# Attention probabilities moved in 32-partition blocks: the order of the block transfers and the length of their pieces

## The chip, the cores and the metric

The kernel runs on one core of a Trainium2 chip. Five engines work beside each other there: TensorE (PE) for matrix products, VectorE (DVE), ScalarE (ACT), GpSimd (POOL) for elementwise work, and SyncE (SP), which in this kernel only issues transfers. The transfers themselves (DMAs) are carried out by 16 DMA engines that all queues share. The metric is the device time of one launch in microseconds; a kernel's time is the median of several runs.

## What is computed

A transformer layer on 8 sequences of 512 tokens with 256 features, all in float32: the normed input goes both through attention with 16 heads of 64 and through a mixture of 16 experts, and both results are added to the input.

```python
xn = _layernorm(x)
# attention, per head
q, k = rope(q), rope(k)
kb = -p * log1p(a * abs(pos_k - pos_q))
attn = softmax(q @ k.T / 8 + kb)
out = (attn @ v) heads joined @ out_w.T
# experts: each token goes to its best one, at most 256 tokens each
h = relu(dispatched @ w1[e]); expert_out = h @ w2[e]
x + attention + gate * expert_out[token]
```

## The kernel before

The attention runs in 32 steps, `s`. A step is a group of four heads (`g = s // 8`) on one sequence (`b = s % 8`), and it falls into two pairs of heads. Each pair is worked in four units of 128 queries (`qc`), two units to a loop body; the body's number is `d`, so a pair takes two bodies. The order of all instructions is written out by hand in the loop over `d` from line 850 on; nothing is reordered afterwards. Each engine, and SyncE's queue of transfers, executes its instructions strictly in that order.

For one pair the data goes this way. `score` (line 610) multiplies queries and keys on PE, adds the distance bias on DVE (line 631) and exponentiates on ACT (line 635). The result stays in a tile `z` with queries on the partitions. The product with the values needs keys on the partitions, so the probabilities must be transposed. `turn` (line 640) does that within blocks of 32 by 32, on DVE. What is left is to move whole blocks between groups of 32 partitions, and this is done by transfers in `move` (line 646): 16 of them for a pair, one for each pair of a source group `qi` and a destination group `g`, from `z` to a tile `pt`. All 16 are issued on SyncE. After the first four a small transfer stores the softmax's reciprocal sums to DRAM (`rd`), and after all 16 two more load them back, broadcast (`rb`). Two pairs later `attend` (line 708) multiplies `pt` with the values, and `attended` (line 720) scales by `rb`. The very last pair is transposed on PE instead (`turn_last`, line 673), so there are 63 moves with 1008 block transfers in all.

Before the change a `z` tile holds, within a partition, first the head of the pair `j`, then the key group `g`, then the key block `c`, then the query unit `qc`, then 32 numbers. A block transfer therefore finds, in each of its 32 source partitions, two pieces of 512 numbers (2048 bytes), one for each head. `pt` is laid out the same way.

SyncE's queue carries more than the blocks. In each step it also loads the partial output (`y`, line 736) and stores it (`yd` or `out`, line 742), loads the normed input two steps ahead (`xnT`, line 235), and during the experts' stage loads their weights (`w`, lines 471 and 480) and stores their results (`eo`, line 538). At the end of a step's second body `load_normed` is called just before `move`. The other queue of transfers, GpSimd's, carries gathers and the first loads and stores.

The buffers: three `z` tiles, two `pt` tiles, two `xnT` tiles, two `y` tiles. A move can be issued when the last `turn` of its pair is done and the `pt` tile of two pairs before has been read by `attend`.

The stages in time: up to about 160 us start-up and norming, to 360 us attention alone with the routing of tokens, to about 1050 us attention with the experts' products in between, then attention with the gathering of the experts' results.

Of the kernel before, what the change touches and what calls it, by code (L numbers as in the profile page):

```python
# [9 lines left out]
F32 = mybir.dt.float32  # L10
# [3 lines left out]
ALU = mybir.AluOpType  # L14
# [3 lines left out]
B, S, DM, H, D = 8, 512, 256, 16, 64  # L18
E, F = 16, 1024
P = 128  # L20
NTOK = B * S
NT = NTOK // P
TB = S // P
# [3 lines left out]
GC = HG * D  # L27
XB = 2
KBW = 2 * S - P
ROT = [(i + 16) % 32 for i in range(32)]  # L30


@with_exitstack
def attention_and_experts(
# [13 lines left out]
    nc = tc.nc  # L48
# [11 lines left out]
    zpool = ctx.enter_context(tc.tile_pool(name="zpool", bufs=3))  # L60
    ptpool = ctx.enter_context(tc.tile_pool(name="ptpool", bufs=2))
# [62 lines left out]

    dist = const.tile([P, TB, KBW // P, 32], F32, name="dist")

    def bias_tables(g, pair, stage):

        for j in range(2):
            h = g * HG + 2 * pair + j  # L130
            if stage == 0:
                kb[h] = kbpool.tile([P, TB, KBW // P, 32], F32, tag="kb", name=f"kb_{h}")
                nc.scalar.activation(
# [16 lines left out]
    for i in range(2):  # L150
# [11 lines left out]
    nc.gpsimd.iota(  # L162
        dist, pattern=[[32, TB], [P, KBW // P], [1, 32]], base=-(S - P),
        channel_multiplier=-1, allow_small_or_imprecise_dtypes=True,
# [399 lines left out]
    def project_qk(s, pair, part, turn_too=True):  # L564
# [8 lines left out]
        sh = rope.tile([P, S], F32, tag="sh", name=f"sh_{s}_{pair}_{part}", bufs=3)  # L573
        nc.vector.stream_shuffle(sh, ps, ROT)  # L574
        t = qkpool.tile([P, S], F32, tag=f"qk{part}{pair}", name=f"t_{s}_{pair}_{part}")
# [34 lines left out]
    def score(s, pair, qc):  # L610

        g = s // B
        q, k = qk[s, pair, 0], qk[s, pair, 1]
        if qc == 0:
            zts[s, pair] = zpool.tile([P, 2, TB, TB, TB, 32], F32, tag="z", name=f"z_{s}_{pair}")
            sums[s, pair] = small.tile([P, 2, TB], F32, tag="sums", name=f"sums_{s}_{pair}")
        sc = [ps_sc.tile([P, S], F32, tag="sc", name=f"sc_{s}_{pair}_{qc}_{j}") for j in range(2)]
        for j in range(2):
            r = slice(j * D, (j + 1) * D)
            nc.tensor.matmul(  # L620
                sc[j].rearrange("p (g c k) -> p g c k", g=TB, k=32),
                q[r, qc * P : (qc + 1) * P],
                k[r, :].rearrange("p (c g k) -> p g c k", g=TB, k=32),
                start=True, stop=True,
            )
        st = small.tile([P, 2], F32, tag="st", name=f"st_{s}_{pair}_{qc}")
        for j in range(2):
            z = zts[s, pair][:, j, :, :, qc, :]
            bias = kb[g * HG + 2 * pair + j][:, :, TB - 1 - qc : 2 * TB - 1 - qc, :]

            nc.vector.tensor_tensor_reduce(  # L631
                z, sc[j].rearrange("p (g c k) -> p g c k", g=TB, k=32), bias, -0.125, 3.0e38,
                ALU.add, ALU.min, st[:, j : j + 1],
            )
            nc.scalar.activation(  # L635
                z, z, AF.Exp, bias=st[:, j : j + 1], scale=-1.0,
                accum_out=sums[s, pair][:, j, qc : qc + 1],
            )

    def turn(s, pair, qc):  # L640

        for j in range(2):
            z = zts[s, pair][:, j, :, :, qc, :]
            nc.vector.transpose(z, z)  # L644

    def move(s, pair):


        z = zts.pop((s, pair))
        inv = inverse[(2 * s + pair) % 2]  # L650
        nc.vector.reciprocal(inv[:, : 2 * TB], sums.pop((s, pair)).rearrange("p j c -> p (j c)"))
        turned = small.tile([P, 32], F32, tag="turned", name=f"turned_{s}_{pair}", bufs=2)
        nc.vector.transpose(turned, inv)
        pt = ptpool.tile([P, 2, TB, TB, P], F32, tag="pt", name=f"pt_{s}_{pair}")
        rd = rdram.tile([TB, 32, 32], F32, tag="rd", name=f"rd_{s}_{pair}")
        for qi in range(TB):
            for g in range(TB):
                nc.sync.dma_start(  # L658
                    pt[g * 32 : (g + 1) * 32, :, qi].rearrange("p j c q -> p j (c q)"),
                    z[qi * 32 : (qi + 1) * 32, :, g].rearrange("p j c q k -> p j (c q k)"),  # L660
                )
            if qi == 0:
                nc.sync.dma_start(rd.rearrange("a c q -> (a c) q"), turned)
        rb = rope.tile([P, TB, P], F32, tag="rb", name=f"rb_{s}_{pair}")
        for j in range(2):
            nc.sync.dma_start(
                rb[j * D : (j + 1) * D],
                rd[:, j * TB : (j + 1) * TB, :].rearrange("a c q -> a (c q)").partition_broadcast(D),
            )
        pts[s, pair] = pt  # L670
        norms[s, pair] = rb

    def turn_last(s, pair, qc):

        if qc == 0:
            pts[s, pair] = zpool.tile([P, 2, TB, S], F32, tag="z", name=f"pt_{s}_{pair}")
        rs = small.tile([P, 2], F32, tag="rs", name=f"rs_{s}_{pair}_{qc}")
        nc.vector.reciprocal(rs, sums[s, pair][:, :, qc])
        for j in range(2):
            zn = rope.tile([P, S], F32, tag="sh", name=f"zn_{s}_{pair}_{qc}_{j}", bufs=3)  # L680
            nc.vector.tensor_scalar(
                zn.rearrange("p (c g k) -> p g c k", g=TB, k=32),
                zts[s, pair][:, j, :, :, qc, :], rs[:, j : j + 1], None, ALU.mult,
            )
            ps = ps_mm.tile([P, TB, P], F32, tag="mm", name=f"zt_{s}_{pair}_{qc}_{j}")
            for kc in range(TB):
                nc.tensor.transpose(ps[:, kc, :], zn[:, kc * P : (kc + 1) * P], ident)
            nc.scalar.copy(pts[s, pair][:, j, :, qc * P : (qc + 1) * P], ps)
# [19 lines left out]
    def attend(s, pair):  # L708
        avs[s, pair] = av = ps_av.tile([P, S], F32, tag="av", name=f"av_{s}_{pair}")
        for kc in range(TB):  # L710
            for j in range(2):
                c0 = pair * P + j * D
                nc.tensor.matmul(  # L713
                    av[j * D : (j + 1) * D, :].rearrange("p (a q) -> p a q", q=P),
                    vals[s][:, kc, c0 : c0 + D], pts[s, pair][:, j, :, kc, :],
                    start=(kc == 0), stop=(kc == TB - 1),
                )
        del pts[s, pair]
# [113 lines left out]
    turn_by(nc.vector, k0[2], k0[0], k0[1], slice(0, S))  # L832
    keep_warm(14)
    score(*units[0])
    score(*units[1])
    turn_by(nc.gpsimd, q0[2], q0[2], q0[1], slice(2 * P, S))
    bias_tables(0, 1, 1)
# [12 lines left out]
    for d in range(duos):  # L850
        s, dd = divmod(d, TB)
        g, b = divmod(s, B)
        pair, half = divmod(dd, 2)
# [5 lines left out]
        if d + 1 < duos:  # L859
            score(*units[2 * d + 2])  # L860
            score(*units[2 * d + 3])
        was = divmod((d - 5) // 2, 2) if half and d >= 5 else None
        if was:
            attend(*was)
# [16 lines left out]
        if d == duos - 1:  # L881
            attended(*was)
            project_out(s - 1, 0)
            project_out(s - 1, 1)
            store_y(s - 1, True)
        (turn_last if final else turn)(*units[2 * d])
        if was and d < duos - 1:
            attended(*was)
# [6 lines left out]
        if dd in (0, 1):  # L895
            project_v(s, dd)
        (turn_last if final else turn)(*units[2 * d + 1])
        if dd == 1 and 4 <= s + 2 < steps:
            load_normed(s + 2)
        if half and not final:  # L900
            move(s, pair)
# [44 lines left out]
        for bb in range(2):  # L946
            k = d - late - 6 * bb - 4
# [8 lines left out]
        for bb in (B - 2, B - 1):  # L956
            k = d - duos + 6 - (bb - B + 2)
# [14 lines left out]
        if b == 0 and g > 0 and dd == 0:  # L972
            bias_tables(g, 1, 1)
    attend(s, 0)
    attended(s, 0)
    for i2 in range(2):
# [56 lines left out]
```

## Time and profile before

| | us |
|---|---|
| median of 3 runs | 1273.08 |
| lowest and highest | 1268.95, 1273.43 |
| the profiled execution, its own time | 1280.13 |
| its span in the profile | 1278.4 |

The page of the profile gives the span in 40 slices; each digit is a share in tenths, 9 for 90% or more:

```profile
PE   8799999999999999999999999999999999999867
DVE  7998897999866556566556566655665568878762
PEclk9899998999999999999999999999999999999989
DMA  4589998888788898878786887877768768999985
```

It gives the transfers of each queue (packets, megabytes, and their time as a share of that of 16 engines), and the chain of work that ended last, by engine:

```profile
q1 hardware_dynamic: 177104, 240.98, 73.6%
q0 software_dynamic: 6368, 20.99, 6.0%
...
PE 71%; DMA 13%; DVE 6%; SPq 5%; ACT 3%; issue 1%; POOL 1%; ACTq 0%; DVEq 0%
```

Queue q1 is SyncE's, q0 GpSimd's. "SPq" is time of SyncE's own instructions, which only issue. The rows of issues read: what is moved, by which queue, how often, KB each, and the median time from issue to landing:

```profile
pt<-z SPq DMA_DIRECT2D x1008, 128.0 KB, 3.2
w<-in_w SPq DMA_DIRECT2D x64, 512.0 KB, 7.4
rb<-rd SPq DMA_DIRECT2D x126, 128.0 KB, 4.1
xnT<-xnd SPq DMA_DIRECT2D x28, 512.0 KB, 5.9
yd<-y SPq DMA_DIRECT2D x26, 512.0 KB, 5.2
y<-yd SPq DMA_DIRECT2D x24, 512.0 KB, 6.8
```

The block transfers are 1008 of about 1400 issues and half of all bytes that the queue moves (1008 x 128 KB of 241 MB).

### The profile page before, as it was taken

How to read it: one execution, taken by the hardware profiler on the slowest of the kernel's cores; microseconds unless marked ns; L12 is line 12 of the kernel's file. 1: busy time of each engine (PE TensorE's matmuls, PEld its weight loads, DVE VectorE, ACT ScalarE, POOL GpSimd, SP SyncE). 2: the span in 40 equal slices, each digit the busy share in tenths (PEclk: the TensorE clock that was granted, in tenths of full speed). 3: DMA queues.
4: the chain of work that ended last, by engine and by line, in shares of the span. 5: the costliest groups of instructions: out<-in, count | busy, mean ns of one | idle time of the engine just before them, and what ended most of it. 6: DMA issues, size and time to landing. Idle time of an engine off the chain costs nothing.

```text
span 1278.4 us, 17383 instructions
## 1 busy us (share of the span) xinstructions
PE 1219.7 (95%) x5070; PEld 670.1 (52%) x5070; DVE 893.5 (70%) x2265; ACT 611.7 (48%) x1425; POOL 617.4 (48%) x614
## 2 busy tenths in 40 slices
PE   8799999999999999999999999999999999999867
PEld 5344444444455565655556565555656554444434
DVE  7998897999866556566556566655665568878762
ACT  6566653466443343445533444443446435555551
POOL 5766654455543343334433344433435334686840
PEclk9899998999999999999999999999999999999989
DMA  4589998888788898878786887877768768999985
GB/s 133 144 209 245 263 229 211 199 199 207 198 221 211 235 238 234 210 198 212 205 217 166 240 203 213 222 209 193 188 195 214 198 156 200 209 227 228 214 229 143
DMA packets 184670, 264.15 MB, mean 207 GB/s; under 512 B 32176, under 2 KB 96448, under 8 KB 184576
## 3 DMA queue, kind: packets, MB, share of 16 engines
q1 hardware_dynamic: 177104, 240.98, 73.6%
q0 software_dynamic: 6368, 20.99, 6.0%
q10 hardware_dynamic: 1104, 1.07, 0.2%
q8 instruction: 41, 0.67, 0.2%
q14 instruction: 53, 0.43, 0.1%
HBM read 99.39 MB, written 31.44 MB: 102 GB/s over the span
## 4 chain that ended last, share of the span: by engine, by line
PE 71%; DMA 13%; DVE 6%; SPq 5%; ACT 3%; issue 1%; POOL 1%; ACTq 0%; DVEq 0%
PE sc L620 13%; PE qk L570 13%; PE av L713 12%; PE po L752 8%; PE v L597 8%; PE ph L515 8%; PE po L530 7%; DMA xnT<-xnd 5%; SPq L658 4%; DMA pt<-z 4%; DMA w<-in_w 3%; DVE z L631 2%; DVE z L644 1%; ACT z L635 1%; ACT xn L245 1%
## 5 line engine op out<-in xcount | busy, mean ns | idle before, releaser
L583 POOL TENSOR_TENSOR t<-t,cos_t 128x512 f32<-128x512 f32 (+1 forms) x126 | 161.3, 1280 | 556.0 <-ACT t L579 555.8
L635 ACT ACTIVATE z<-z,st 128x512 f32<-128x512 f32 x512 | 363.3, 711 | 44.8 <-DVE st L631 36.4
L631 DVE CUSTOM_DVE_ANT_1 z<-sc,kb 128x512 f32<-128x512 f32 x512 | 322.6, 686 | 35.3 <-PE sc L620 26.5
L644 DVE STREAM_TRANSPOSE z<-z 128x512 f32<-128x512 f32 x504 | 319.8, 682 | 0.0
L570 PE MATMUL qk<-xnT,wq 128*128 128x512 f32 x512 | 247.8, 607 | 12.6 <-DMA xnT<-xnd 8.1
L620 PE MATMUL sc<-t,t 64*128 64x512 f32 x1024 | 255.3, 617 | 0.7 <-DVE t L585 0.7
L713 PE MATMUL av<-pt,v 128*64 128x512 f32 x1008 | 235.5, 610 | 9.1 <-DMA pt<-z 8.3
L579 ACT COPY t<-qk 128x512 f32<-128x512 f32 x125 | 73.2, 585 | 341.8 <-DVE sh L574 341.8
L574 DVE LOAD_MASK_SELECT sh<-qk x128 | 1.8, 14 | 241.4 <-PE qk L570 239.4
L620 PEld LDWEIGHTS sc<-t,t 64*128 64x128 f32 x1024 | 88.5, 186 | 155.0 <-issue 127.7
L585 POOL TENSOR_TENSOR t<-t,sh 128x512 f32<-128x512 f32 (+1 forms) x126 | 160.5, 1274 | 9.9
L584 POOL TENSOR_TENSOR sh<-sh,sin_t 128x512 f32<-128x512 f32 (+1 forms) x126 | 161.0, 1278 | 0.0
L713 PEld LDWEIGHTS av<-pt,v 128*64 128x64 f32 x1008 | 69.2, 139 | 167.0 <-issue 136.6
L570 PEld LDWEIGHTS qk<-xnT,wq 128*128 128x128 f32 x512 | 94.4, 192 | 101.5 <-issue 69.0
L752 PE MATMUL po<-wo,o 128*128 128x256 f32 x512 | 124.3, 386 | 0.2 <-DVE o L723 0.2
L597 PE MATMUL v<-wq,xnT 128*128 128x256 f32 x512 | 124.1, 385 | 0.0
L530 PE MATMUL po<-w,hT 128*128 128x256 f32 x512 | 120.5, 383 | 3.5 <-DMA w<-in_w 2.5
L515 PE MATMUL ph<-xdT,w 128*128 128x256 f32 x512 | 118.8, 382 | 2.2 <-ACT eot L536 1.4
L752 PEld LDWEIGHTS po<-wo,o 128*128 128x128 f32 x512 | 94.5, 190 | 36.4 <-issue 11.1
L597 PEld LDWEIGHTS v<-wq,xnT 128*128 128x128 f32 x512 | 94.7, 190 | 35.8 <-DVE z L644 14.6
L515 PEld LDWEIGHTS ph<-xdT,w 128*128 128x128 f32 x512 | 95.6, 190 | 27.7 <-ACT z L635 4.9
L530 PEld LDWEIGHTS po<-w,hT 128*128 128x128 f32 x512 | 95.0, 190 | 28.7 <-issue 9.4
(147 smaller groups left out, 828.3 us busy)
## 6 DMA issues: line engine op xcount, KB each, us to landing
pt<-z SPq DMA_DIRECT2D x1008, 128.0 KB, 3.2
w<-in_w SPq DMA_DIRECT2D x64, 512.0 KB, 7.4
rb<-rd SPq DMA_DIRECT2D x126, 128.0 KB, 4.1
xnT<-xnd SPq DMA_DIRECT2D x28, 512.0 KB, 5.9
yd<-y SPq DMA_DIRECT2D x26, 512.0 KB, 5.2
y<-yd SPq DMA_DIRECT2D x24, 512.0 KB, 6.8
xrd<-xn POOLq DMA_DIRECT2D x8, 512.0 KB, 6.8
xnd<-xnT POOLq DMA_DIRECT2D x8, 512.0 KB, 7.8
```

The lines of the kernel that those rows point to most:

```text
L515: nc.tensor.matmul(ph[:, i, :], held["w1", e, fc // 4][:, mc, (fc % 4) * P : (fc % 4 + 1) * P], xdT[:, mc, :], start=(mc == 0), stop=(mc = ...
L530: nc.tensor.matmul(po[:, c, :], hT[:, fc, c * P : (c + 1) * P], held["w2", e, fc // 4][:, fc % 4, :], start=(fc == 0), stop=(fc == F // P ...
L570: nc.tensor.matmul(ps, wq[:, mc, c0 : c0 + P], xnTs[s][:, mc, :], start=(mc == 0), stop=(mc == 1),)
L583: eng.tensor_tensor(t[:, c], ps[:, c], cos_t[:, c], ALU.mult)
L584: eng.tensor_tensor(sh[:, c], sh[:, c], sin_t[:, c], ALU.mult)
L597: nc.tensor.matmul(ps[:, i, :], xnTs[s][:, mc, c0 : c0 + P], wq[:, mc, 2 * GC :], start=(mc == 0), stop=(mc == 1),)
L620: nc.tensor.matmul(sc[j].rearrange("p (g c k) -> p g c k", g=TB, k=32), q[r, qc * P : (qc + 1) * P], k[r, :].rearrange("p (c g k) -> p g c ...
L631: nc.vector.tensor_tensor_reduce(z, sc[j].rearrange("p (g c k) -> p g c k", g=TB, k=32), bias, -0.125, 3.0e38, ALU.add, ALU.min, st[:, j : ...
L635: nc.scalar.activation(z, z, AF.Exp, bias=st[:, j : j + 1], scale=-1.0, accum_out=sums[s, pair][:, j, qc : qc + 1],)
L644: nc.vector.transpose(z, z)
L713: nc.tensor.matmul(av[j * D : (j + 1) * D, :].rearrange("p (a q) -> p a q", q=P), vals[s][:, kc, c0 : c0 + D], pts[s, pair][:, j, :, kc, : ...
L752: nc.tensor.matmul(ps[:, i, :], oTs[pair][:, c0 : c0 + P], wot[:, pair, :], start=(pair == 0), stop=(pair == 1),)
```

## The change

The two layouts get the head `j` further inside, so that a block is one piece of 1024 numbers (4096 bytes) in each partition, in the source and in the destination. The 16 blocks are issued in a new order. Before, `qi` ran outside and `g` inside: eight transfers from the lower half of the partitions, then eight from the upper. Now a list names them by turns: (0,0), (2,2), (0,1), (2,3), (0,2), (2,0), (0,3), (2,1), and the same with 1 and 3 as sources. Every transfer reads from the other half than the one before it, and writes to the other half. The store of `rd` still follows the fourth block. All that reads or writes `z` and `pt` is indexed to suit; no operation is added or removed.

```diff
+BLOCKS = [
+    b for q in range(2) for g in range(4) for b in ((q, g), (q + 2, (g + 2) % 4))
+]
...
-            zts[s, pair] = zpool.tile([P, 2, TB, TB, TB, 32], F32, tag="z", name=f"z_{s}_{pair}")
+            zts[s, pair] = zpool.tile([P, TB, TB, 2, TB, 32], F32, tag="z", name=f"z_{s}_{pair}")
...
-            z = zts[s, pair][:, j, :, :, qc, :]
+            z = zts[s, pair][:, :, :, j, qc, :]
...
-        pt = ptpool.tile([P, 2, TB, TB, P], F32, tag="pt", name=f"pt_{s}_{pair}")
+        pt = ptpool.tile([P, TB, TB, 2, P], F32, tag="pt", name=f"pt_{s}_{pair}")
         rd = rdram.tile([TB, 32, 32], F32, tag="rd", name=f"rd_{s}_{pair}")
-        for qi in range(TB):
-            for g in range(TB):
-                nc.sync.dma_start(
-                    pt[g * 32 : (g + 1) * 32, :, qi].rearrange("p j c q -> p j (c q)"),
-                    z[qi * 32 : (qi + 1) * 32, :, g].rearrange("p j c q k -> p j (c q k)"),
-                )
-            if qi == 0:
+        for i, (qi, g) in enumerate(BLOCKS):
+            nc.sync.dma_start(
+                pt[g * 32 : (g + 1) * 32, qi].rearrange("p c j q -> p (c j q)"),
+                z[qi * 32 : (qi + 1) * 32, g].rearrange("p c j q k -> p (c j q k)"),
+            )
+            if i == 3:
                 nc.sync.dma_start(rd.rearrange("a c q -> (a c) q"), turned)
...
-                    vals[s][:, kc, c0 : c0 + D], pts[s, pair][:, j, :, kc, :],
+                    vals[s][:, kc, c0 : c0 + D], pts[s, pair][:, :, kc, j, :],
```

More of the change, by code (lines that the diff above doesn't have):

```diff
@@ L642, in turn @@
         for j in range(2):
-            z = zts[s, pair][:, j, :, :, qc, :]
+            z = zts[s, pair][:, :, :, j, qc, :]
             nc.vector.transpose(z, z)
@@ L682, in turn_last @@
                 zn.rearrange("p (c g k) -> p g c k", g=TB, k=32),
-                zts[s, pair][:, j, :, :, qc, :], rs[:, j : j + 1], None, ALU.mult,
+                zts[s, pair][:, :, :, j, qc, :], rs[:, j : j + 1], None, ALU.mult,
             )
```

## The prediction

> **What bounds the kernel now.** I read the page's busy shares first, then a table of busy time by stage, then who TensorE (PE) waited for in each stage, then SyncE's queue (SPq) in order of time.
>
> ```profile
> PE 1219.7 (95%) x5070; PEld 670.1 (52%) x5070; DVE 893.5 (70%) x2265; ACT 611.7 (48%) x1425; POOL 617.4 (48%) x614
> 160.00:360.00 200.00, 191.23 (x775) 89.63 (x772) 184.25 (x475) 105.55 (x251) 105.79 (x91) 0.98 0.85 207
> 360.00:1120.00 760.00, 753.93 (x3082) 441.99 (x3082) 473.46 (x1153) 336.15 (x775) 314.43 (x260) 1.00 0.79 208
> 1120.00:1240.00 120.00, 107.04 (x410) 51.51 (x407) 94.23 (x238) 66.88 (x168) 88.04 (x71) 0.97 0.94 227
> ```
>
> Columns of the last three: stretch, length, busy us of PE, weight loads, DVE, ACT, POOL, then granted clock, DMA share, GB/s. In the middle, where the experts run between the heads, PE is idle 6 us of 760: nothing can be won there. It is idle 8.8 us of 200 before and 13 us of 120 after. The waits of PE from 1120 to 1262 us, and the largest from 160 to 360:
>
> ```profile
> PE av L713 <- DMA pt<-z: 8.3, 4, 3.5
> PE zt L687 <- ACT pt L688: 6.1, 2, 5.9
> PE qk L570 <- DMA xnT<-xnd: 2.2, 2, 1.2
> ...
> PE qk L570 <- DMA xnT<-xnd: 5.9, 3, 3.7
> ```
>
> All of these go back to transfers; the 5.9 us ACT wait is for a z buffer that a move is still reading (ACT pt L688 waited 5.7 us for DMA pt<-z). The queue that issues them, in the late stage, and what it waited for from 1060 to 1260:
>
> ```profile
> 1093.54 2.58 SPq L658 DMA_DIRECT2D pt<-z  x4
> 1096.22 0.53 SPq L663 DMA_DIRECT2D rd<-turned  x1
> 1096.79 9.92 SPq L658 DMA_DIRECT2D pt<-z  x12
> 1106.76 1.30 SPq L666 DMA_DIRECT2D rb<-rd  x2
> 1108.16 0.55 SPq L742 DMA_DIRECT2D yd<-y  x1
> 1108.81 0.38 SPq L235 DMA_DIRECT2D xnT<-xnd  x1
> ...
> SPq L658 <- DMA y<-yd: 7.5, 5, 2.2
> SPq L658 <- DMA xnT<-xnd: 6.1, 3, 2.1
> SPq L658 <- DMA pt<-z: 4.2, 7, 1.4
> ...
> L658 SPq DMA_DIRECT2D pt<-z x1008: 585/597/2221, 47.5 to 1256.7; - x168
> L235 SPq DMA_DIRECT2D xnT<-xnd x28: 320/339/1117, 116.1 to 1177.2; - x28
> ```
>
> The queue has no gap between one move and the next. The first row to the next pair's first row (1109.28) is 15.7 us a pair. PE needs less: between v projections at 1075.06 and 1104.46 in the chain two pairs passed in 29.4 us, 14.7 a pair, with PE never idle. So before 360 us and after 1060 SyncE's queue is as slow as PE or slower; from 1126 to 1193 it takes 16.9 a pair, and PE waits.
>
> Where do 15.7 us go? Sixteen block issues at 0.597 plus 0.044 between are 10.3; rd about 0.6, two rb 1.3, y or yd with half an xnT 0.9: 13.1. The other 2.6 (about 3.8 late) are stalls. The semaphores in the operands show why: SyncE's transfers use eight in rotation, so each waits until the one eight places earlier has landed. Eight places are about 5 us; y lands after 6.8, xnT after 7.3.
>
> They land late because block transfers occupy the engines. In the packet records a 2048-byte packet takes 81 to 84 ns in the fastest tenth, but 147 at the median and 150 to 160 inside a move. A block is 64 packets, four per engine: 4 x 0.150 plus a semaphore packet, 0.61 us, against an issue every 0.64. A backlog left by a 512 KB load is hardly drained during the sixteen blocks. Their landing is 2.5 us at the median in the middle and 4.4 after 1060.
>
> [...] 131072 bytes per 0.64 us are 205 GB/s, and packets take nearly twice their unobstructed time. [...] 22096 semaphore packets on queue 1 are 16 for each of its 1381 transfers. [...] the trace has 159 ns for 4096 bytes against 2 x 84.
>
> **The change part by part.** *One piece of 4096 bytes.* 64 packets of 2048 become 32 of 4096, two per engine. Unobstructed that saves 168 - 159 = 9 ns per pair of packets, 18 ns a block. [...] I expect 2 x 290 against 4 x 150: 0.58 for 0.60. The issue may get cheaper, as the pattern loses a dimension: [128 partitions, 1 piece] costs 326 ns (fastest xnT after an idle stretch, yd 328), [128, 2] 374 to 390 (eo, w1). That difference of 50 ns is the nearest row; 32-partition blocks cost 585 even after idleness, for a reason the trace doesn't show. Bounds: no gain, since 627 to 633 is the price after a pause whatever precedes, and 260 ns if the block falls to xnT's price. I take 40 ns: 0.64 us a pair.
>
> *By turns.* Source and destination change half at every issue. The same sixteen blocks move, the same wait (last turn of z) stands ahead of the first, attend needs all sixteen either way, and rd stays after the fourth block. With no backlog a block is nearly finished when the next is issued, so alternation does little. [...] Packet starts within a block are spread by about 0.2 us of 0.64[...]. Bounds of a block's service: 0.58 (no overlap) and 0.34 (2 x 159 plus semaphore). I take 0.47 in a backlog; 1.5 us of backlog then drains in nine blocks (0.17 each at an issue every 0.64) or twelve (0.13 at 0.60) instead of never. Large landings come some 1 to 1.5 us sooner, which halves the stalls: 1.3 us a pair early, 1.9 late.
>
> *Strides.* z's 128-byte runs go from 512 to 1024 bytes apart, pt's 512-byte runs from 2 to 4 KB. The scores on DVE take 686 ns strided against about 690 for contiguous y L757 of the same size; av matmuls 592 at the fastest, equal to the contiguous qk. I cost this at nothing. DVE is busy 184 of 200 us early, so if a longer stride did cost 5% on z's rows, about 4 us would show there.
>
> **Sum.** SyncE per pair: early 13.1 - 0.6 + 1.3 = 13.8 against about 15.2 for PE; late 13.1 - 0.6 + 1.9 = 14.4 against 14.7. The queue falls just behind PE's pace and stops setting it. PE's idle ledger, gap by gap, where a transfer ended the wait: early 0.8 (rb) + 3.7 + 1.0 + 1.2 (xnT) + 1.5 (ACT behind such a load) = 8.2; middle 3.3 (expert weights); late 2.2 + 1.3 + 3.5 + 1.3 (pt) + 1.1 + 1.2 (xnT) + 5.9 (the z buffer) = 16.5. Together 28. The clock was granted at half speed for 6.8 us at 194, 3.4 at 1146, 3.4 at 1214 and 10.2 at 1242, each following such a gap; leaving out the part where PE was idle anyway, that loses 3.4 + 1.7 + 1.7 + 2.9 = 9.7. All of it would be 38. I take half, 19: single late loads stay, POOL's gathers keep the DMA busy late, and next in line are DVE early (184 of 200) and the first heads' start-up, which no block touches. 1280.1 for the profiled execution becomes 1261. That execution lies 7 us above the median of the runs shown, some of it perhaps in these very waits, so I subtract 18 from the median 1273.1: 1255.
>
> **The rivals.**
> 1. *The halves overlap fully, or the issue falls to xnT's price.* SyncE then needs at most its 13.1 us a pair and only PE remains: 85% of 38, less the same 1, so 1273 - 31 = 1242. For it: 84 against 150 ns, and 585 against 326. Against: [...] a fast issue was seen with 128 partitions only. 0.18.
> 2. *Engines stay in step and the issue costs the same.* Packets drain 5% faster, stalls shrink by a tenth: 1273 - 3 = 1270. For it: issue and service are already matched at 0.64 and 0.61. 0.20.
> 3. *Slower: long packets in step outlast the issue.* In a busy stretch late (1098 to 1106) seven 4096-byte packets took 333 ns at the median against 159 for 2048. At 2 x 333 plus semaphore a block needs 0.69, more than 0.64; from that point DMA, not SyncE, paces a move: 16 x 0.05 = 0.8 us more each, on some 25 moves of the early and late stages 20 us, so 1293. Against: only seven packets, mostly with HBM at one end. 0.12.
>
> **How the numbers follow.** The forecast, 1255, has 0.50; its own range is 1246 to 1265. Reaching to rival 1 and through most of rival 2 gives 1238 to 1273, which leaves out the slow side and little else. Half a percent, 6.4 us, is about what a measurement here can tell from none. Faster: nearly all of the forecast (0.49), rival 1 (0.18), a little of rival 2 (0.03), 0.70. Same: the rest of rival 2 and of the forecast, 0.18. Slower: 0.12.
>
> **What would show it.** Right: 64,512 packets of 2048 bytes replaced by 32,256 of 4096, with many near 160 ns; queue 1's share well below 73.6%; block landings after 1060 nearer 2.5 than 4.4; SyncE's waits for xnT and y halved; gaps on SPq between moves; PE's late waits for pt mostly gone; the half-speed spells at 194 and 1214 gone. The issue's share: the block issue's median below 597. Wrong: packets at 300 ns throughout with SPq still closed up (rival 2), or moves longer than 10.3 us without stalls (rival 3).

## The result and the profile after

The changed kernel took 1263.15 us at the median of seven runs (1259.97 to 1268.44), against 1273.43 for seven runs of the kernel before; the ratio is 0.9925, with an interval of 0.9905 to 0.9945. In a later series, with six runs of the changed kernel and 24 of the one before, it was 1260.82 against 1277.21, 0.9875 (0.9852 to 0.9898). The change makes the kernel 10 to 16 us faster. The forecast was 1255, its range 1238 to 1273.

The profiled executions differ by more, 1280.13 against 1259.97. First the line of PE, DVE, ACT and POOL from the page after, and the table of busy time by stage, with the columns and stretches of before (the changed kernel's line numbers are three or four higher):

```profile
PE 1214.7 (97%) x5070; PEld 669.1 (53%) x5070; DVE 892.5 (71%) x2265; ACT 611.8 (49%) x1425; POOL 618.1 (49%) x614
```

```profile
160.00:360.00 200.00, 198.42 (x814) 92.28 (x810) 190.20 (x490) 109.45 (x261) 109.92 (x94) 1.00 0.86 218
360.00:1120.00 760.00, 757.59 (x3102) 445.71 (x3100) 478.61 (x1167) 340.20 (x784) 322.17 (x265) 1.00 0.78 208
1120.00:1240.00 120.00, 103.15 (x410) 51.15 (x408) 86.48 (x216) 63.07 (x156) 76.97 (x63) 0.95 0.92 234
```

In the early stage PE was idle for 8.8 us of 200 and is now idle for 1.6. In the middle it was idle for 6 and is now for 2.4. The early figure isn't steady: in a second profile of the changed kernel (`after_again`, below) PE was idle for 5.5 us there, 3.7 of them behind xnT, so 1.6 is not what every execution gives:

```profile
160.00:360.00 200.00, 194.45 (x793) 91.74 (x791) 187.12 (x480) 105.61 (x250) 105.37 (x92) 0.99 0.82 209
```

The late stretch can't be compared line with line, since the kernel ends 20 us sooner and the stretch now reaches further into the last pairs. PE's waits there, from 1120 to 1262 us:

```profile
PE zt L690 <- ACT pt L691: 5.9, 2, 5.7
PE zt L690 <- DVE zn L684: 3.9, 2, 2.5
PE qk L574 <- ACT early L781: 1.9, 1, 1.9
PE av L716 <- DMA rb<-rd: 1.8, 1, 1.8
PE av L716 <- DMA pt<-z: 1.3, 1, 1.3
PE qk L574 <- DMA xnT<-xnd: 1.2, 1, 1.2
```

The direct waits for blocks went from 8.3 us to 1.3, and those for xnT from 2.2 to 1.2. The wait for the z buffer that a move still reads (the first row) hardly changes, from 6.1 us to 5.9. SyncE's queue in the same late stage, in order of time, and what it waited for from 1060 to 1260; then the rows of the block issues and of the queue's transfers:

```profile
1079.05 2.46 SPq L661 DMA_DIRECT2D pt<-z  x4
1081.60 0.53 SPq L666 DMA_DIRECT2D rd<-turned  x1
1082.18 9.22 SPq L661 DMA_DIRECT2D pt<-z  x12
1091.44 1.30 SPq L669 DMA_DIRECT2D rb<-rd  x2
1092.84 0.55 SPq L745 DMA_DIRECT2D yd<-y  x1
1093.48 0.38 SPq L239 DMA_DIRECT2D xnT<-xnd  x1
1093.95 3.00 SPq L661 DMA_DIRECT2D pt<-z  x4
```

```profile
SPq L661 <- DMA y<-yd: 6.5, 5, 1.8
SPq L661 <- DMA xnT<-xnd: 5.5, 4, 1.9
```

```profile
L661 SPq DMA_DIRECT2D pt<-z x1008: 507/589/2004, 47.5 to 1235.8; - x168
```

```profile
q1 hardware_dynamic: 144848, 240.98, 72.5%
```

The queue is still without a gap between moves. A pair takes 14.9 us here, and over the nine pairs from 1079.05 to 1225.32 it takes 16.25; in the kernel before the nine pairs from 1093.54 to 1245.69 took 16.9. So the late stage is paced by SyncE as before, only less slowly. In the early stage the queue is closed up too; there a pair takes 15.6 us (thirteen moves from 165.08 to 352.26) and took 16.0 (twelve from 168.78 to 344.89). The block's issue is 78 ns cheaper at the fastest but only 8 at the median. The number of packets on the queue fell by 32,256, as half of the pieces must, and yet the share of the engines' time fell by one point only: each block packet moves twice as much and takes nearly twice as long (265 ns in the mean against 142, within the moves).

### The profile page after: what moved, and what is told of

Read it like the earlier page. It is cut to its first block, busy times and chain, and to the rows that moved or that the text cites. A ratio compares the mean times of both kernels' runs of the same rounds, so it can differ in the third digit from the quotient of the medians.

```text
span 1258.3 us, 17383 instructions
## 1 busy us (share of the span) xinstructions
PE 1214.7 (97%) x5070; PEld 669.1 (53%) x5070; DVE 892.5 (71%) x2265; ACT 611.8 (49%) x1425; POOL 618.1 (49%) x614
## 3 DMA queue, kind: packets, MB, share of 16 engines
q1 hardware_dynamic: 144848, 240.98, 72.5%
## 4 chain that ended last, share of the span: by engine, by line
PE 76%; DVE 8%; DMA 7%; SPq 4%; POOL 2%; ACT 2%; issue 1%; ACTq 0%; DVEq 0%; POOLq 0%
PE sc L624 15%; PE qk L574 14%; PE av L716 14%; PE ph L519 9%; PE po L534 9%; PE v L601 7%; PE po L755 7%; SPq L661 3%; DVE z L635 3%; DMA pt<-z 2%; DVE z L648 2%; DMA rd<-turned 1%; DMA xnT<-xnd 1%; DMA xnd<-xnT 1%; DMA out<-early 1%
## 5 line engine op out<-in xcount | busy, mean ns | idle before, releaser
L716 PE MATMUL av<-pt,v 128*64 128x512 f32 x1008 | 232.1, 602 | 3.7 <-DMA rb<-rd 1.8
L601 PEld LDWEIGHTS v<-wq,xnT 128*128 128x128 f32 x512 | 94.7, 190 | 35.8 <-DVE z L648 13.8
```

Of the source, the lines that this page charges most:

```text
L601: nc.tensor.matmul(ps[:, i, :], xnTs[s][:, mc, c0 : c0 + P], wq[:, mc, 2 * GC :], start=(mc == 0), stop=(mc == 1),)
L716: nc.tensor.matmul(av[j * D : (j + 1) * D, :].rearrange("p (a q) -> p a q", q=P), vals[s][:, kc, c0 : c0 + D], pts[s, pair][:, :, kc, j, : ...
```

## The experiments

Each kernel's ratio is to the kernel before in runs on the same chip. From the packet records of each profile I also give the mean time of the moves' packets, per 2048 bytes, counted from 3 us after a move's first issue to 1.5 us after its last: it is 141.9 ns in the kernel before and 132.5 in the changed one (132.1 in its second profile, the only sign of how steady this mean is). And I give SyncE's stalls: the sum of its waits that a transfer ended at the lines of `move`. They are 98 us in the kernel before and 75 in the changed one (81 in its second profile).

**One half of the change at a time.** The piece alone, and the turns alone:

```diff
 # piece_only: the changed kernel with the old order
+BLOCKS = [(qi, g) for qi in range(4) for g in range(4)]
 # order_only: the old layout with the new order
-        for qi in range(TB):
-            for g in range(TB):
+        for i, (qi, g) in enumerate(BLOCKS):
```

> The layout of the changed kernel (one piece of 4096 bytes) with the old order of the blocks, sources 0,0,0,0,1,1,1,1 and so on. If the gain comes from the cheaper issue after a pause (559 for 633 ns) and the fewer packets, this keeps most of it: 0.993 to 0.995 of before. If it comes from the turns, nothing is left: 0.998 to 1.001, with 4096-byte packets of the moves near 300 ns. If long packets in step cost more than two short ones, it is slower than before, 1.002 to 1.01.

Measured: 1270.54 us, 0.9975 (0.9964 to 0.9986); packets 135.9 ns.

> The old layout (two pieces of 2048 bytes) with the new order by turns. If the turns carry the gain: 0.992 to 0.995, median of the 2048-byte packets clearly below 147 ns. If the piece carries it: 0.998 to 1.001, packets as before. The first issue of a move stays at 633 ns in both.

Measured: 1266.03 us, 0.9943 (0.9929 to 0.9957); packets 136.4 ns. Both halves help. The turns are worth about twice the piece, and their product, 0.9918, is the whole change's 0.9925 within its interval. The piece's gain lies between the two outcomes I had named. They seem to help in different ways. The stalls are 71 us in order_only, as low as in the changed kernel, but 102 in piece_only, no lower than before. So the turns shorten the stalls and the piece by itself does not; a move's sixteen issues add up to 10.1 us in piece_only and 10.4 before, which may be its way, but no run isolates that.

**Which side of the turns counts.** In the changed kernel's list the sources change half at every block, but the destinations do not quite: the fourth and fifth, the eighth and ninth, and the twelfth and thirteenth block write to the same half. In the next kernels the piece stays and only the list of blocks differs. `source_turns` changes the source's half at each block and the destination's after four; `dest_turns` changes the destination's half at every block without exception, with eight blocks in a row from one half of the sources; `dest_runs8` writes eight blocks to the lower half and then eight to the upper, with sources by turns.

```diff
+BLOCKS = [(q + 2 * h, g) for q in range(2) for g in range(4) for h in range(2)]   # source_turns
+BLOCKS = [(q, g + 2 * h) for q in range(4) for g in range(2) for h in range(2)]   # dest_turns
+BLOCKS = [(q + 2 * h, g) for g in range(4) for q in range(2) for h in range(2)]   # dest_runs8
```

> The changed kernel, with sources by turns (0,2,0,2 ...) but each two following blocks going to the same destination group, so writes stay in one half for four blocks. [...] it is as fast as the changed kernel (0.992 to 0.994); if the writing side binds as well, half or more of the gain of the turns is lost (0.996 to 1.0).

Measured: 1277.51 us, 1.0026 (1.0012 to 1.0040), slower than either outcome I had named, of which the first was for the reading side alone to bind.

> The changed kernel, with destinations by turns (0,2,1,3) but four blocks in a row from one source group, so reads stay in one half for eight blocks. If only the writing side binds: 0.992 to 0.994. If the reading side binds, it is like the layout alone with the old order.

Measured: 1266.04 us, 0.9936 (0.9922 to 0.9949).

> The changed kernel once more, on the same chip as the next two: 0.991 to 0.995 of before.

Measured: 1260.82 us, 0.9875 (0.9852 to 0.9898), faster than I expected.

> The changed kernel with the destination group outside: eight blocks in a row into the lower half, then eight into the upper, while the sources change half at every block. If the writing side is what binds, this is the worst order: slower than two in a row (piece_only 0.9975) and at least as slow as four in a row (source_turns 1.0026): 1.002 to 1.008, packets of the moves at 280 ns or more. If reading matters as much, its alternating sources bring it to 0.995 to 0.999.

Measured: 1283.45 us, 1.0053 (1.0034 to 1.0073). All with pieces of 4096 bytes, in the order of the number of blocks that go to one half in a row:

| kernel | in a row, destination | in a row, source | packet, ns per 2048 bytes | queue's share of the engines | stalls, us | ratio |
|---|---|---|---|---|---|---|
| changed | 1 (three times 2) | 1 | 132.5 | 72.5% | 75 | 0.9925, 0.9875 |
| dest_turns | 1 | 8 | 131.6 | 71.6% | 75 | 0.9936 |
| piece_only | 2 | 8 | 135.9 | 73.3% | 102 | 0.9975 |
| source_turns | 4 | 1 | 139.4 | 74.6% | 116 | 1.0026 |
| dest_runs8 | 8 | 1 | 144.3 | 75.9% | 128 | 1.0053 |

The rows come from three series, each ratio against the kernel before in its own. Time, packets and stalls follow the destination's column alone. Turns on the reading side bring nothing that these runs can tell: with eight sources in a row the packets are as short as with one. The order of the writes is what matters, and grouping them is enough to make the kernel slower than before.

One thing stays open. In source_turns two blocks in a row, and in dest_runs8 four, also go to the same 32 partitions, so in these two the half and the group are not told apart. From dest_turns to piece_only no group is repeated, and there the second block in a row to one half already costs 4.3 ns.

**Is the narrow span the reason?** If a block's packets are slow because all of it lies within 32 partitions, those of a transfer over all 128 should not be. Such a transfer can't do the transposition of blocks, but it moves the same bytes:

```diff
-        for i, (qi, g) in enumerate(BLOCKS):
+        for g in range(TB):
             nc.sync.dma_start(
-                pt[g * 32 : (g + 1) * 32, qi].rearrange("p c j q -> p (c j q)"),
-                z[qi * 32 : (qi + 1) * 32, g].rearrange("p c j q k -> p (c j q k)"),
+                pt[:, g].rearrange("p c j q -> p (c j q)"),
+                z[:, g].rearrange("p c j q k -> p (c j q k)"),
             )
```

> The changed kernel, but each move is 4 transfers over all 128 partitions, 4096 bytes of each, which copy each partition to itself: all bytes move, but not between the groups of partitions, so the transposition of blocks is left out and the output is not the reference's. [...] packets of the moves fall from about 265 to about 160 ns, issues to about 0.33 us, and the time to 0.975 to 0.983 of before, at or below half_bytes. If packets are slow because reading and writing in the same memory is slow, they stay above 220 ns.

Measured: 1248.48 us, 0.9781 (0.9753 to 0.9808). The page's row for the queue, and the early and late rows of the table by stage:

```profile
q1 hardware_dynamic: 132752, 240.93, 54.9%
```

```profile
160.00:360.00 200.00, 198.42 (x815) 92.51 (x813) 190.90 (x494) 110.30 (x264) 110.08 (x95) 1.00 0.64 227
...
1120.00:1240.00 120.00, 113.06 (x469) 55.82 (x466) 86.95 (x220) 63.64 (x159) 79.76 (x64) 0.97 0.65 226
```

The column to look at is the one before the last: at about the same rate in the last column the engines are busy 0.64 and 0.65 of the time, against 0.86 and 0.92 in the changed kernel. The moves' packets of 4096 bytes take 159 ns at the median and 162 in the mean, 81.0 per 2048 bytes. So copying within the on-chip memory isn't what makes a block's packets slow; the narrow span of partitions is. This run also copies each partition to itself, but so do the four blocks with `qi` equal to `g`, and theirs are no exception: counted off in the order of their starts, in the twelve moves of loads_pool (below) where that can be done, their means were 199 to 285 ns, those of the other twelve blocks 226 to 268. Why a narrow span slows them isn't shown. The run's time can't be put down to the packets alone, since it also has four issues for sixteen. The issue did not fall to the 0.33 us that I expected: 710 ns at the median, for a reason that this run doesn't show (each transfer is four times as large).

**Issues or engines?** Two kernels halve one of them each:

```diff
 # half_issues: 8 transfers of 8192 bytes a partition
+        for i, (qi, g) in enumerate(BLOCKS[:8]):
...
+                pt[g * 32 : (g + 1) * 32, qi // 2 * 2 : qi // 2 * 2 + 2].rearrange("p a c j q -> p (a c j q)"),
+                z[qi * 32 : (qi + 1) * 32, g // 2 * 2 : g // 2 * 2 + 2].rearrange("p a c j q k -> p (a c j q k)"),
 # half_bytes: 16 transfers of 2048 bytes a partition
+                pt[g * 32 : (g + 1) * 32, qi, 0:2].rearrange("p c j q -> p (c j q)"),
+                z[qi * 32 : (qi + 1) * 32, g, 0:2].rearrange("p c j q k -> p (c j q k)"),
...
+                    vals[s][:, kc, c0 : c0 + D], pts[s, pair][:, :, kc % 2, j, :],
```

> The changed kernel, but each move is 8 transfers of 8192 bytes a partition (256 KB) instead of 16 of 4096: all bytes move, half of the issues. The blocks land in wrong places, so the output is not the reference's; no time depends on the values. If SyncE's issuing (0.63 us a block) paces the moves, a move takes about 7 us instead of 12.4 and the late waits go: 0.975 to 0.985 of before. If the DMA engines pace them [...], a move's end is hardly sooner, stalls take the place of issues, and the time stays at the changed kernel's 0.990 to 0.994.

Measured: 1256.27 us, 0.9865 (0.9831 to 0.9899). A move takes 7.4 us from its first issue to the end of its last, instead of 12.4, and the stalls are 20 us instead of 75.

> The changed kernel, but each of the 16 transfers moves only 2048 bytes a partition (key blocks 0 and 1; the product with the values reads these twice), so half of the bytes are left out and all issues stay. If issuing paces the moves: the issue stays near 0.59 us and the time near the changed kernel's, 0.988 to 0.993, the rest from shorter stalls. If the DMA engines pace them: 0.975 to 0.985.

Measured: 1251.42 us, 0.9822 (0.9788 to 0.9856), with stalls of 25 us. Their rows of block issues, half_issues first, and half_bytes' row for the queue:

```profile
L661 SPq DMA_DIRECT2D pt<-z x504: 507/607/1872, 47.1 to 1219.3; - x168
```

```profile
L661 SPq DMA_DIRECT2D pt<-z x1008: 507/588/2312, 47.7 to 1228.6; - x168
```

```profile
q1 hardware_dynamic: 144848, 174.92, 48.9%
```

Halving the bytes leaves the issue at 588 ns. So it is not the engines that hold the issue at 0.59 us; a run of blocks, one after the other, costs SyncE that much with 2048 or 4096 bytes in a piece. half_issues came out between the two outcomes I had named. half_bytes' time lies in the range named for the engines, though its issue stayed where the other outcome had it. By its ratio half_bytes (0.9822) lies below both measurements of the changed kernel (0.9925 and 0.9875); half_issues (0.9865) can't be told from the second. Both took away most of the stalls, one by fewer issues and one by fewer bytes, so issues and engines both stand in the way, and the stalls join the two.

**The stalls behind large loads.** SyncE's loads of y and xnT go to GpSimd's queue, in the changed kernel (`loads_pool`) and in the one before (`loads_pool_old`):

```diff
-        nc.sync.dma_start(xnT, xnd[s % B])
+        nc.gpsimd.dma_start(xnT, xnd[s % B])
...
-        nc.sync.dma_start(
+        nc.gpsimd.dma_start(
             ys[s], x[b].rearrange("(n p) d -> p n d", p=P) if g == 0 else yd[b]
```

> The changed kernel, with the loads of y and xnT (52 of 512 KB and 8 more from x) issued on GpSimd's queue instead of SyncE's. If what is left is SyncE's stalls behind these loads (xnT 22.5 us, y 22.5 us of waits in the changed kernel's profile), they go, and the time is 0.983 to 0.989 of before. If the DMA engines' time is what is left, or GpSimd is delayed by it: 0.991 to 0.996.

Measured: 1257.81 us, 0.9870 (0.9843 to 0.9897).

> The kernel before, with the same loads on GpSimd's queue, blocks unchanged. If the change gained by shortening SyncE's stalls behind large loads, this gains about as much by itself, 0.988 to 0.994, and the change on top of it (loads_pool) adds less than the 0.75% it is worth alone. [...]

Measured: 1261.67 us, 0.9903 (0.9876 to 0.9929). What SyncE waited for most in loads_pool:

```profile
SPq L661 <- DVE z L648: 261.7, 52, 10.1
SPq L661 <- DVE turned L657: 36.5, 1, 36.5
SPq L661 <- DMA pt<-z: 24.6, 39, 1.5
```

The first of these rows in the changed kernel, and the wait at its load of xnT, which loads_pool no longer has in this queue:

```profile
SPq L661 <- DVE z L648: 89.2, 16, 8.7
SPq L239 <- PE v L601: 110.1, 16, 10.1
```

The queue of loads_pool in the late stage:

```profile
1095.01 2.45 SPq L661 DMA_DIRECT2D pt<-z  x4
1097.56 0.53 SPq L666 DMA_DIRECT2D rd<-turned  x1
1098.13 8.47 SPq L661 DMA_DIRECT2D pt<-z  x12
1106.65 1.33 SPq L669 DMA_DIRECT2D rb<-rd  x2
1108.87 2.51 SPq L661 DMA_DIRECT2D pt<-z  x4
```

Now there is a gap before the move (1107.98 to 1108.87), and the longest total wait is for the last `turn` on DVE: 261.7 us, where the changed kernel waits 89.2 for it and 110.1 for PE just ahead of it, together 199. SyncE is further ahead of the compute engines. Moving two kinds of load gains, in the kernel before, about as much as the whole change, without touching a block. On top of it the change is worth 3.9 us of 1261.7, 0.3%, less than half of what it is worth alone; if the gain were in the engines' shorter time, 0.6 to 0.9% was expected. So more than half of the change's gain overlaps with what the moved loads had cost, which is their stalls and their own issues on SyncE. It may also be that little is left to gain: PE is idle for only 2 us of the early stage in either of these two kernels. What the remaining part is isn't shown. Of the kernels that compute everything, loads_pool has the lowest median, 1257.81 against 1263.15 and 1260.82 for the changed kernel, but it wasn't run in a series with the changed kernel.

## Why the prediction was right, and where it was off

**The bound.** Right. SyncE's queue and the engines behind it set the pace before 360 us and after 1060, and the middle could gain little: its idle time fell by 3.7 us of 6, and the rest came from the two ends.

**The pace.** Wrong. The queue was to need 13.8 us a pair early and 14.4 late, to fall behind PE's pace and to stop setting it. It needs 15.6 and 16.25, and is still closed up in both stages. Of the signs that were named, the late waits for pt mostly went, a half-speed spell of the clock at 194 us is gone, and the block issue's median fell. The gaps between moves, the halved waits for xnT (30.6 to 22.5 us) and y (21.3 to 22.5), the packets near 160 ns and a share well below 73.6% did not come.

**The sum against the profile.** PE's idle time, the span less its busy time, fell from 58.7 to 43.6 us, by 15.1. Its busy time fell from 1219.7 to 1214.7, since only 13.4 us of it ran at half clock, where 22.5 had. Together that is 20.1, where the prediction took 19 (half of 28 idle and of 9.7 for the clock), and the profiled execution came out at 1260 for a predicted 1261. The kinds of time were right, but taking half of them was a judgement, and it went with a pace that the queue did not reach, so the near hit is in part luck. In the second profile idle time is 48.1 us. (One clock term was a little large: PE was busy for 5.5 us of the spell at 194, which loses 2.8 and not 3.4.)

**From there to the median.** The profiled execution of before lay 7 us above the median, the prediction said that some of it might lie in these very waits, and then it took off only 1. The medians differ by 10.3 us in one series and 16.4 in the other, so the 18 were too many. That the 7 us were such waits would fit: 38 us of idle and clock in a run that was 7 us slow would be about 31 in a typical one, and half of it 15. It isn't shown, since only that one execution of the kernel before was profiled.

**The terms.** Three were mis-sized. The issue: 40 ns a block were expected. The first block of a move became 74 ns cheaper (633 to 559), and one behind a wait or behind the store of rd 78 (585 to 507), but in a run of blocks the median went from 597 to 589. The service in a backlog: 0.47 us were my estimate between bounds of 0.58 and 0.34, and no trace had shown that turns would shorten it at all. At the measured mean of 265 ns for 4096 bytes it is 0.53 and the semaphore; the turns shorten packets by 2.5 to 4%, the piece by 3 to 4%. The stalls: they were to be halved. They went from 98 us to 75, a quarter less.

**The rivals.** Rival 2 was right that packets hardly get faster (6.6% for the 5% it named) and that the issue costs nearly the same. It was wrong on the time, 1270: a tenth off the stalls was expected and a quarter came, and 0.9 us went from each of 63 moves (13.3 to 12.4 at the mean). In this kernel, where many such transfers stand in a row on the queue that sets the pace, the turns shortened a packet by 2.5 to 4% and alone brought 0.57%. Rival 1's 1242 is near what all_ports reaches, 1248, with the block transposition and most issues left out. The changed kernel goes between a third and a bit more than a half of the way there (10 and 16 of 29 us). Rival 3, slower by long packets, is refuted by piece_only. A slower order exists, but it is grouped writes that make it so, which I had not named.

**What was costed at nothing.** The longer strides: the scores' row on DVE has a mean of 686 ns in both kernels, the transposes 682, and the fastest av matmul 592. Right.

## What to carry to other kernels

When many narrow transfers follow each other on one queue, look at the half of the partitions that each one writes. Here, by turns was best; against two in a row, turns brought about 0.4% and runs of eight cost 0.8%. Before that, look at what else shares the queue: large loads among many small transfers, with eight semaphores in rotation, stalled it here (the changed kernel waited 22.5 us each for xnT and for y), and moving those loads to the other queue, which had little to do (5.8% of the engines' time), was worth about as much as the change (0.9903 in the kernel before). When the sum is made from one profiled execution, ask where that execution lies among the runs: its distance from the median may lie in the very waits that the change is to remove.

## What the runs showed of the hardware

- The order of destinations alone, with the same transfers and bytes, moves a packet's mean time from 131.6 to 144.3 ns per 2048 bytes (one to eight blocks in a row to one half of the partitions), and SyncE's stalls from 75 to 128 us. The order of sources showed no effect beside it (131.6 ns with eight in a row, 132.5 by turns).
- A packet of 4096 bytes between partitions takes 162 ns in the mean when a transfer spans 128 partitions and 265 when it spans 32. Both have 16 semaphore packets to a transfer, as many as the core has DMA engines: the changed kernel's queue has 22096 for 1381 transfers and all_ports' 10000 for 625.
- Issuing a 32-partition block costs 507 ns with one piece and 585 with two behind a wait or behind the small store of rd, but 588 to 597 in a run of blocks with either, and with 2048 or 4096 bytes in the piece. What the price in a run is made of stays open.
